# A state-space scan with a running attention behind it: attention in two halves, VectorE's side work between product and scan, decays six states ahead

## The chip, the cores and the metric

One core of one Trainium2 chip runs the whole program in one launch. The metric is the device time of an execution in microseconds. The core has five engines that run side by side and meet through semaphores: TensorE (PE in the profile, matmuls; PEld is its weight load), VectorE (DVE), ScalarE (ACT), GpSimd (POOL) and SyncE (SP), which here issues all transfers. All of them take their instructions in the order of the program.

## What is computed

The input x is 16 images of 128 channels by 64 x 64 positions. Layer 0 adds a selective state-space block (Mamba) to it, layer 1 an attention over prefixes, and after it a layer of experts. Cut to what matters here:

```python
u = group_norm(x) as tokens                      # 16 x 4096 x 128
xs, z = split(u @ W_in)
xc = silu(causal_conv(xs))                       # 256 channels, 4 taps
dt, Bm, Cm = split(xc @ W_xproj)                 # 8, 16 and 16 columns
delta = softplus(dt @ W_dt + b_dt)
A = -exp(A_log)                                  # 256 x 16
# over the 4096 tokens, for each channel d and each of 16 states n:
#   h[n] = exp(delta * A[n]) * h[n] + delta * xc * Bm[n]
#   y    = sum over n of h[n] * Cm[n]
x = x + ((y + xc * D) * silu(z)) @ W_out         # with rows and columns of the image swapped
t = x as tokens
k, v = silu(layer_norm(t) @ W_kv.T)              # 8 heads of 128
s = q . k                                        # one score per head and token
m = running max of s;  e = exp(s - m)
t = t + mean over heads of cumsum(e * v) / cumsum(e)
t = t + expert layer (top 8 tokens per expert)
```

## The kernel before

Each image has 4096 tokens; the kernel takes them in blocks of L = 512, 8 blocks to an image, 128 blocks in all. One step k of the main loop (line 600) works on four blocks at once: it scans block k (`cur`), finishes block k-1 (`prev`: gate, output projection, residual), prepares block k+1 (`nxt`: convolution, x projection, delta), and runs the attention of block m = k - 9 (`LAG`, line 566), whose image is then complete. `mp_` is the attention block of the step before, `mn` that of the next. So the first nine steps have no attention, and after step 127 some ten steps have attention alone.

A step has 16 slots n, one for each state. In a slot, `scan` (line 343) makes on DVE the product `bx` of delta times x (`du`) with row B of state n, in PSUM, and then two linear scans of 512 tokens (two halves of the channels) into `h`; POOL multiplies h with row C of the state into the tile of the decay (`da`); two slots later PE turns this tile by an identity and sums it in PSUM (`add_y`, line 364). The rows B and C come from memory, repeated over the partitions, by a transfer `load_bc` four states ahead (line 332, four buffers). `decay` (line 337) makes exp(delta * A[n]) on ACT, up to `LEAD` = 5 states ahead, in eight buffers. `keep_state` (line 358) copies the last token's state on ACT; h has two buffers.

Everything else of a step is spread over the slots by `slot(n)` (lines 611 to 703), an order written by hand: the wrappers `PE`, `DVE`, `ACT`, `POOL` (class `InOrder`, line 23) keep each engine's instructions in the order in which the code calls them. Transfers go through `nc.sync` and are placed by the framework's scheduler. In a slot the order is: scan, load_bc, the state copy of the slot before, `slot(n)`, `add_y(n-2)`, decays, loads.

The attention of a block: `ln_center`, `ln_scale`, `ln_apply` normalise; `key` makes one head's keys; `score` the scores in the one bank of pool `acc`; `score_max` the running max and four copies of rows into `lh`; `score_exp` e; `score_sum` the running sum and e turned into `e1`; `score_log` the logarithm of the sum and eight copies of rows into `rh`; `value` half the heads' values for one chunk of 128 tokens; `weights` (line 511) forms from lh and rh, by a matmul of 5 rows and an Exp on ACT, the 128 x 128 weights of a chunk for all heads; `attend` multiplies them with the values into `o` (pool `acc` again) and sums the chunk for `carry`; `attend_before` adds what comes from earlier chunks; `finish` adds the result to the image and stores it. PSUM has three banks for short results (pool `ps`), one for scores and o, two for y and two for bx.

In the slots before: keys 0 to 2, score_max 3, score_exp 4, score_sum 5, score_log 6, values 7 to 9, ln_center 10, weights of chunks 0 to 3 in slots 11 to 14 and attend of chunks 0 to 2 in 12 to 14, attend of chunk 3 and finish in slots 0 and 1 of the next step. `gate` is in slot 3, `residual` in 5, `delta_x` (du of the next block) in slot 15 behind the scan, `gn_stats` in 12, and `gn_end`, a short chain through DVE, PE and ACT, in slot 14 of one step in eight.

Of the kernel before, what the change touches and what calls it, by code (L numbers as in the profile page):

```python
# [39 lines left out]
def conv_attn_hybrid(ctx: ExitStack, tc: tile.TileContext, x, w_in, conv_w, conv_b, w_xproj, w_dt, b_dt,  # L40
# [72 lines left out]
    with ExitStack() as st:  # L113
# [94 lines left out]
        dap = st.enter_context(tc.tile_pool(name="dap", bufs=8))  # L208
# [133 lines left out]

        def scan(k, n):
# [5 lines left out]
            bt, da = w.pop(("bc", n)), w["da", n]  # L349
            bx = bps.tile([P, NH2, L], F32, tag="bx", name="bx")  # L350
            DVE.tensor_tensor(bx, w["du"], bc(bt[:, 0:1, :], [P, NH2, L]), ALU.mult)
# [55 lines left out]

        def residual(k):

            w = blocks.pop(k)  # L410
            J = L // HH
            xv = res[w["b"]].rearrange("p (i j) -> p j i", j=WW)[:, w["i"] * J : (w["i"] + 1) * J, :]
            DVE.tensor_tensor(xv, xv, w["o"].rearrange("p (j i) -> p j i", j=J), ALU.add)
# [6 lines left out]
        def ln_center(m):  # L420
            b, i, xs = where(m)
            s = att[m] = dict(cen=bank("cen_ps"))
            PE.matmul(s["cen"], cmat, xs, start=True, stop=True)
            s["sq"] = short("sq")
            ACT.activation(s["sq"], s["cen"], AF.Square)
# [9 lines left out]
        def ln_apply(m):  # L435
            s = att[m]
            s["xn"] = a1.tile([P, L], F32, tag="xn", name="xn", bufs=2)
# [18 lines left out]
        def score_max(m):  # L456
# [10 lines left out]

            for u in range(2):
# [9 lines left out]
        def score_sum(m):  # L478
# [4 lines left out]
            DVE.tensor_copy(gn[b]["den"], s["mx"][:, L - 1 : L])  # L483
            et = bank("et_ps")
# [38 lines left out]
        def attend(m, c):  # L523
# [3 lines left out]
            if c == 0:  # L527
                s["o"] = acc.tile([P, L], F32, tag="acc", name="ao_ps")
            cols, v, wm = bass.ts(c, P), s.pop(("v", c)), s.pop(("wm", c))
            for h in range(HD):  # L530
                g, j = divmod(h, 4)

                PE.matmul(s["o"][:, cols], v[:, h, :], wm[:, j // 2, j % 2, g, :], start=(c == 0 and h == 0),
# [16 lines left out]
        def attend_before(m, c):  # L550
            s = att[m]
            if m % NBLK or c:
                PE.matmul(s["o"][:, bass.ts(c, P)], carry[:, (c - 1) % 4, :], s["e"][:, bass.ts(c, P)], start=False,
                          stop=True, skip_group_check=True)

        def finish(m):
            b, i, xs = where(m)
            s = att.pop(m)
            DVE.scalar_tensor_tensor(xs, s["o"], 1.0 / HD, xs, ALU.mult, ALU.add)
            nc.sync.dma_start(t2_d[b, :, bass.ts(i, L)], xs)  # L560
# [6 lines left out]
        LEAD = 5  # L567
# [30 lines left out]
        decays(0, 0, 5)  # L598

        for k in range(NK + LAG + 1):  # L600
# [10 lines left out]
            def slot(n):  # L611

                if n == 0:
                    if mp_ is not None:
                        attend(mp_, 3)
                        attend_before(mp_, 2)
# [4 lines left out]
                    if mp_ is not None:  # L621
                        carry_on(mp_, 2)
                if n == 1:
                    if mp_ is not None:
                        attend_before(mp_, 3)
# [4 lines left out]
                    if mp_ is not None:  # L630
                        carry_on(mp_, 3)
                        finish(mp_)
                    if m is not None:
# [14 lines left out]
                if n == 3:  # L648
# [4 lines left out]
                    if prev is not None:  # L653
                        gate(prev)
                if n == 4:
                    if prev is not None:
                        out_proj(prev)
                    if m is not None:
                        score_exp(m)
                    if nxt is not None:  # L660
                        conv(nxt, 0)
                if n == 5:
                    if prev is not None:
                        residual(prev)
                    if m is not None:
                        score_sum(m)
                    if nxt is not None:
                        conv(nxt, 1)
                if n == 6 and m is not None:
                    score_log(m)  # L670
                if n == 7:
                    if nxt is not None:
                        conv_silu(nxt)
                    if cur is not None:
                        gate_silu(cur)
                    if nxt is not None:
                        xproj(nxt)
                if 7 <= n <= 9 and m is not None:
                    for x in ((0, 1), (2, 3, 4), (5, 6, 7))[n - 7]:
                        value(m, x // 2, x % 2)  # L680
                if n == 9 and nxt is not None:
                    delta(nxt)
                if n == 10:
                    load_exp()
                    if mn is not None:
                        ln_center(mn)
                if n == 11 and mn is not None:
                    ln_scale(mn)
                if m is not None:
                    if 11 <= n <= 14:  # L690
                        weights(m, n - 11)
                    if n >= 12:
                        c = n - 12
                        if c < 3:
                            attend(m, c)
                        if c == 1:
                            attend_before(m, 0)
                            carry_on(m, 0)
                        if c == 3:
                            attend_before(m, 1)  # L700
                            carry_on(m, 1)
                if n == 13 and mn is not None:
                    ln_apply(mn)

            for n in range(N):
                if cur is not None:
# [6 lines left out]
                    if n == N - 1 and nxt is not None:  # L713
                        delta_x(nxt)
                if prev is not None and n == 0:
                    keep_state(prev, N - 1)
                slot(n)
                if cur is not None and n >= 2:
                    add_y(cur, n - 2)
                if 3 <= n <= 6 or n >= 10:  # L720
# [4 lines left out]
                if n == 0 and i == 1 and cur is not None:  # L725
# [166 lines left out]
```

## Time and profile before

| what | value |
|---|---|
| median of 3 runs | 13192.64 us (13183.42 to 13194.23) |
| the profiled execution | 13180.11 us, span 13178.4 us |
| PE busy | 11484.8 us (87%), mean granted clock 0.886 |
| DVE busy | 9947.5 us (75%) |
| ACT busy | 7080.3 us (54%) |
| POOL busy | 6336.2 us (48%) |
| first du of the loop, last du | 72.3 us, 11108.1 us |
| HBM | 105 GB/s over the span |

The main loop ends near 11,190 us, attention alone runs to about 11,690, and the expert layer takes the rest; the change touches only the main loop and the steps behind it. Line numbers are of little use in the profile: all in-order instructions are recorded in the helper's line 31, so groups are told apart by their tiles (`out<-in`). A few per cent of the records are missing. The costliest groups, each a line of the page's fifth part: the multiply with C on POOL (2048 of 2946 ns), the scans on DVE (4096 of about 1260 ns), the products bx on DVE (2048 of 1509 ns), the decays on ACT (4096 of 711 ns), and on PE the turns of y (16384 of 287 ns), the attention's products (8192 of 336 ns) and the weights (2048 of 728 ns).

### The profile page before, as it was taken

How to read it: one execution, taken by the hardware profiler on the slowest of the kernel's cores; microseconds unless marked ns; L12 is line 12 of the kernel's file. 1: busy time of each engine (PE TensorE's matmuls, PEld its weight loads, DVE VectorE, ACT ScalarE, POOL GpSimd, SP SyncE). 2: the span in 40 equal slices, each digit the busy share in tenths (PEclk: the TensorE clock that was granted, in tenths of full speed). 3: DMA queues.
4: the chain of work that ended last, by engine and by line, in shares of the span. 5: the costliest groups of instructions: out<-in, count | busy, mean ns of one | idle time of the engine just before them, and what ended most of it. 6: DMA issues, size and time to landing. Idle time of an engine off the chain costs nothing. (4 is left out here: it accounts for less than half of the span.)

```text
span 13178.4 us, 153074 instructions
## 1 busy us (share of the span) xinstructions
PE 11484.8 (87%) x55359; PEld 6609.2 (50%) x55359; DVE 9947.5 (75%) x8977; ACT 7080.3 (54%) x12594; POOL 6336.2 (48%) x2590
## 2 busy tenths in 40 slices
PE   5588989889888989898989889888988898988887
PEld 3344555555455545554555555545555555444464
DVE  7988888888888888888888888888888888124422
ACT  4456555656565655566555656565656565432210
POOL 5655555555555555555555555555555555012310
PEclk7689999999999999999989999999999999888975
DMA  4544444444444444444444444444444443011127
GB/s 129 125 112 106 111 106 114 109 107 109 110 108 111 107 106 113 106 113 106 112 103 113 109 109 107 112 109 107 110 105 113 102 112 96 7 48 45 52 81 290
DMA packets 693703, 1400.71 MB, mean 106 GB/s; under 512 B 51072, under 2 KB 89616, under 8 KB 684752
## 3 DMA queue, kind: packets, MB, share of 16 engines
q1 hardware_dynamic: 692944, 1390.92, 40.8%
q8 instruction: 436, 7.14, 0.2%
q14 instruction: 323, 2.65, 0.1%
HBM read 1294.25 MB, written 92.27 MB: 105 GB/s over the span
## 5 line engine op out<-in xcount | busy, mean ns | idle before, releaser
L31 POOL TENSOR_TENSOR da<-h,bct 128x1024 f32<-128x1024 f32 x2048 | 6034.0, 2946 | 5154.1 <-DVE h L31 1812.6
L31 DVE TENSOR_TENSOR_SCAN h<-da,state,bx 128x512 f32<-128x512 f32 x3584 | 4392.4, 1267 | 578.3 <-ACT state L31 389.5
L31 DVE TENSOR_TENSOR bx<-du,bct 128x1024 f32<-128x1024 f32 x2048 | 3090.6, 1509 | 43.8 <-DMA bct<-bcs 2.9
L31 ACT ACTIVATE da<-delta,a_neg 128x512 f32<-128x512 f32 x4096 | 2639.6, 711 | 365.2 <-PE y_ps L31 359.1
L31 PE MATMUL y_ps<-ident,da 128*128 128x128 f32 x16384 | 2280.9, 287 | 154.5 <-POOL da L31 153.5
L31 PEld LDWEIGHTS y_ps<-ident,da 128*128 128x128 f32 x16384 | 1957.4, 148 | 900.4 <-issue 635.3
L31 ACT ACTIVATE wm<-w_ps 128x512 f32<-128x512 f32 x1024 | 608.7, 594 | 1561.7 <-PE w_ps L31 1559.1
L31 PEld LDWEIGHTS ao_ps<-wm,v 128*128 128x128 f32 x8192 | 1268.4, 244 | 346.5 <-issue 346.5
L31 PE MATMUL ao_ps<-wm,v 128*128 128x128 f32 x8192 | 1369.3, 336 | 0.0
L31 PE MATMUL w_ps<-rh,lh 5*128 5x512 f32 x2048 | 1320.7, 728 | 0.0
L31 PE MATMUL xs_ps<-xb,wc 128*128 128x512 f32 x2048 | 987.5, 627 | 304.1 <-DVE xt L31 302.3
L31 PE MATMUL k_ps<-xn,wk 128*128 128x512 f32 x2048 | 988.4, 615 | 55.2 <-DVE carry L31 55.2
L31 ACT ACTIVATE kt<-k_ps 128x512 f32<-128x512 f32 x1024 | 586.9, 602 | 755.3 <-PE k_ps L31 755.3
L31 PE MATMUL v_ps<-wv,xn 128*128 128x512 f32 x2048 | 964.9, 605 | 6.6 <-ACT z L31 3.3
L31 ACT ACTIVATE v<-v_ps 128x512 f32<-128x512 f32 x1024 | 610.4, 598 | 477.1 <-PE v_ps L31 477.1
L107 POOL TENSOR_SCALAR diag<-ident,rstd 128x128 f32<-128x128 f32 x512 | 299.1, 602 | 1164.5 <-DVE rstd L96 1100.1
L31 PEld LDWEIGHTS xs_ps<-xb,wc 128*128 128x128 f32 x2048 | 402.0, 202 | 797.6 <-issue 438.8
L31 DVE TENSOR_TENSOR_SCAN h<-da,bx 128x512 f32<-128x512 f32 x512 | 597.0, 1208 | 88.4 <-ACT state L31 60.1
L31 DVE TENSOR_TENSOR carry<-carry,carry_ps 128x128 f32<-128x128 f32 x496 | 135.9, 274 | 693.0 <-PE carry_ps L31 693.0
L31 PEld LDWEIGHTS k_ps<-xn,wk 128*128 128x128 f32 x2048 | 367.8, 196 | 483.3 <-issue 451.5
L31 ACT COPY state<-h 128x2 f32<-128x2 f32 x1792 | 334.2, 187 | 487.0 <-DVE h L31 486.5
L31 PEld LDWEIGHTS v_ps<-wv,xn 128*128 128x128 f32 x2048 | 363.3, 192 | 453.2 <-issue 430.8
(163 smaller groups left out, 11528.7 us busy)
## 6 DMA issues: line engine op xcount, KB each, us to landing
bct<-bcs SPq DMA_DIRECT2D x2048, 512.0 KB
xs<-in_x_dram SPq DMA_DIRECT2D x128, 256.0 KB
xt<-in_x_dram SPq DMA_DIRECT2D x16, 2048.0 KB
t_d<-xt SPq DMA_DIRECT2D x128, 256.0 KB
t<-t_d SPq DMA_DIRECT2D x64, 512.0 KB
tc<-t_d SPq DMA_DIRECT2D x16, 2048.0 KB
out_dram<-tc SPq DMA_DIRECT2D x16, 2048.0 KB
xb<-in_x_dram SPq DMA_DIRECT2D x112, 257.5 KB
```

Of the source, the lines that this page charges most:

```text
L31: return lambda *args, **kw: self.tc.keep_in_program_order(f(*args, **kw))
L107: nc.gpsimd.tensor_scalar(diag[:, c, :], ident, rstd[:, k : k + 1], None, ALU.mult)
```

## The change

- The product of slot n is taken out of `scan` into `product`. A slot now runs: `before(n)` (only score_sum in slot 7), in slot 0 `delta_x`, the product, in slot 12 `gn_stats`, then `beside(n)` (the former `slot`), then the scans, load_bc and the state copy of the slot before. So the state copy of slot n-1 now follows ACT's work of slot n.
- Attention in two halves: chunks 0 and 1 keep slots 12 to 15 of their step; weights and attend of chunks 2 and 3 go to slots 3 to 5 of the next step. `o` holds two chunks at a time, `finish` runs twice (slots 0 and 7 of the next step), with two stores of 256 columns. The four copies into lh move to slot 5 (`spread_weights`), score_exp to 6, score_sum to 7, the turning of e to 8 (`turn_weights`), score_log with its eight copies to 11, values to slots 8 to 10.
- Convolutions go to slots 6 and 7, conv_silu to 7, gate_silu and xproj to 8, delta and ln_center to 11, the square to 12, ln_apply to 14, out_proj to 5, residual to 6. In the second block of an image the projected output is set aside by an ACT copy and added in slot 11, and the load of the image's residual starts in slot 7.
- Decays run up to six states ahead in nine buffers, in slots 3 to 7 and 12 to 15; xn has one buffer in place of two.

```diff
+        def product(k, n):
+            w = blocks[k]
+            bx = w["bx"] = bps.tile([P, NH2, L], F32, tag="bx", name="bx")
+            DVE.tensor_tensor(bx, w["du"], bc(w["bc", n][:, 0:1, :], [P, NH2, L]), ALU.mult)
...
-            bt, da = w.pop(("bc", n)), w["da", n]
-            bx = bps.tile([P, NH2, L], F32, tag="bx", name="bx")
-            DVE.tensor_tensor(bx, w["du"], bc(bt[:, 0:1, :], [P, NH2, L]), ALU.mult)
+            bt, da, bx = w.pop(("bc", n)), w["da", n], w.pop("bx")
...
+        def set_aside(k):
+            w = blocks[k]
+            o = short("o")
+            ACT.copy(o, w["o"])
+            w["o"] = o
...
-            if c == 0:
+            if c % 2 == 0:
                 s["o"] = acc.tile([P, L], F32, tag="acc", name="ao_ps")
-            cols, v, wm = bass.ts(c, P), s.pop(("v", c)), s.pop(("wm", c))
+            cols, v, wm = bass.ts(c % 2, P), s.pop(("v", c)), s.pop(("wm", c))
...
-        def finish(m):
+        def finish(m, half):
             b, i, xs = where(m)
-            s = att.pop(m)
-            DVE.scalar_tensor_tensor(xs, s["o"], 1.0 / HD, xs, ALU.mult, ALU.add)
-            nc.sync.dma_start(t2_d[b, :, bass.ts(i, L)], xs)
+            s = att[m] if half == 0 else att.pop(m)
+            xs = xs[:, bass.ts(half, L // 2)]
+            DVE.scalar_tensor_tensor(xs, s["o"][:, : L // 2], 1.0 / HD, xs, ALU.mult, ALU.add)
+            nc.sync.dma_start(t2_d[b, :, i * L + half * (L // 2) : i * L + (half + 1) * (L // 2)], xs)
...
-        LEAD = 5
+        LEAD = 6
...
+            def before(n):
+                if n == 7 and m is not None:
+                    score_sum(m)
+            def beside(n):
                 if n == 0:
...
                     if m is not None:
                         key(m, 0), key(m, 1), key(m, 2)
                     if mp_ is not None:
-                        carry_on(mp_, 2)
+                        finish(mp_, 0)
...
+                    if mp_ is not None:
+                        weights(mp_, 2)
                 if n == 4:
+                    if mp_ is not None:
+                        weights(mp_, 3)
+                        attend(mp_, 2)
+                if n == 5:
+                    if m is not None:
+                        spread_weights(m)
                     if prev is not None:
                         out_proj(prev)
+                    if mp_ is not None:
+                        attend(mp_, 3)
+                        attend_before(mp_, 2)
+                        carry_on(mp_, 2)
+                if n == 6:
                     if nxt is not None:
                         conv(nxt, 0)
+                    if mp_ is not None:
+                        attend_before(mp_, 3)
                     if prev is not None:
+                        set_aside(prev) if i == 1 else residual(prev)
+                    if mp_ is not None:
+                        carry_on(mp_, 3)
+                    if m is not None:
+                        score_exp(m)
+                if n == 7:
+                    if mp_ is not None:
+                        finish(mp_, 1)
                     if nxt is not None:
                         conv(nxt, 1)
                         conv_silu(nxt)
+                if n == 8:
                     if cur is not None:
                         gate_silu(cur)
+                    if m is not None:
+                        turn_weights(m)
                     if nxt is not None:
                         xproj(nxt)
...
+                if n == 11:
+                    if nxt is not None:
+                        delta(nxt)
                     if mn is not None:
                         ln_center(mn)
+                    load_exp()
+                    if m is not None:
+                        score_log(m)
+                if n == 12:
+                    if mn is not None:
+                        ln_square(mn)
+                        ln_scale(mn)
+                    if m is not None:
+                        weights(m, 0)
+                if n == 13:
+                    if m is not None:
+                        weights(m, 1)
+                        attend(m, 0)
+                        attend_before(m, 0)
+                if n == 14:
+                    if mn is not None:
+                        ln_apply(mn)
+                    if m is not None:
+                        attend(m, 1)
+                        carry_on(m, 0)
+                if n == 15 and m is not None:
+                    attend_before(m, 1)
+                    carry_on(m, 1)
...
             for n in range(N):
+                before(n)
+                if cur is not None:
+                    if n == 0 and k:
+                        delta_x(k)
+                    product(cur, n)
+                if n == 12 and stat is not None:
+                    gn_stats(*stat)
+                beside(n)
                 if cur is not None:
                     scan(cur, n)
...
                     if n:
                         keep_state(cur, n - 1)
-                    if n == N - 1 and nxt is not None:
-                        delta_x(nxt)
...
-                slot(n)
...
-                if 3 <= n <= 6 or n >= 10:
+                if 3 <= n <= 7 or n >= 12:
                     decays(k, n, 2)
```

## The prediction, made before the changed kernel was run

> **What bounds the kernel now.** First the page's busy shares by slice: VectorE (DVE) 8 tenths and TensorE (PE) 8 to 9 through the loop, so neither is full, and PE's granted clock hangs between 0.8 and 0.9. A mean over such a loop says little, so the second view is a table of windows: one step of the first batch, where attention does not run yet, and one full step (from one BATCH_NORM_STATS2 to the next).
>
> ```profile
> DVE  7988888888888888888888888888888888124422
> PEclk7689999999999999999989999999999999888975
> ...
> 5013.00:5098.00 85.00, 76.55 (x389) 43.66 (x389) 74.00 (x65) 52.54 (x96) 47.09 (x16) 0.93 0.51 110
> 211.00:284.00 73.00, 43.91 (x176) 27.65 (x176) 70.42 (x55) 35.01 (x64) 49.62 (x17) 0.71 0.50 125
> ```
>
> The columns are PE, PE weight load, DVE, ACT, POOL busy, then the clock. Without attention DVE is the bound (70.4 of 73). With it DVE works 74.0 of 85, PE 76.6.
>
> Third, DVE's timeline in an attention-free step, beside POOL's there:
>
> ```profile
> 212.49 1.20 DVE L31 TENSOR_TENSOR du<-delta,xc 128x1024 f32<-128x1024 f32 x1
> 213.72 3.25 DVE L31 TENSOR_TENSOR bx<-du,bct 128x1024 f32<-128x1024 f32 x1
> 217.11 2.45 DVE L31 TENSOR_TENSOR_SCAN h<-da,state,bx 128x512 f32<-128x512 f32 x2
> 219.59 1.23 DVE L31 TENSOR_TENSOR bx<-du,bct 128x1024 f32<-128x1024 f32 x1
> ...
> 231.03 1.26 DVE L31 TENSOR_TENSOR z<-yb_ps,z 128x512 f32<-128x512 f32 x2
> 232.21 2.61 DVE L31 TENSOR_TENSOR bx<-du,bct 128x1024 f32<-128x1024 f32 x1
> ```
>
> The product bx takes 1.23 us directly behind a scan, and 2.6 to 3.25 when other DVE work stands between. POOL's multiply (2.35 us alone, 3.22 when a product got in first) then starts ahead of the product and the product sits it out. That is the cost which the reordering attacks.
>
> Fourth, what PE waited for in the full step, and SyncE's queue there:
>
> ```profile
> PE xs_ps L31 <- DVE xt L31: 2.6, 1, 2.6
> PE z_ps L31 <- ACT xc L31: 2.4, 1, 2.4
> PE o_ps L31 <- DVE z L31: 1.8, 1, 1.8
> PE w_ps L31 <- ACT rstd L31: 0.7, 1, 0.7
> PE var_ps L31 <- ACT sq L31: 0.6, 1, 0.6
> PE yb_ps L31 <- ACT kt L31: 0.4, 1, 0.4
> ```
>
> ```profile
> 5069.43 1.28 SPq L497 DMA_DIRECT2D rh<-mx  x2
> 5075.95 0.36 SPq L335 DMA_DIRECT2D bct<-bcs  x1
> 5076.38 3.66 SPq L497 DMA_DIRECT2D rh<-mx  x6
> ```
>
> The PE waits sum to 8.5 us. The queue shows that eight rh copies cost about 5 us of issue, and that a bct load, which waits for POOL to free its buffer, holds up those behind it (5.2 us here, harmless, as the weights follow 14 us later).
>
> **PE's account of a step, before.** From starts to next starts in PE's timeline at full clock: 17 turns y of 0.87 = 14.8; 4 weight pairs (w) of 2.74 = 11.0; 4 attends with their carry sums, 1.88 + 0.58 = 9.8; keys 6.9, values 6.9, convolution 6.9; scores 2.0, out projection 1.8, yb 1.0, z 1.7, dbl 1.7, dt 1.9, cen 0.9, var 1.0, et 0.5, four carried products 0.9. Sum 69.6. With 8.5 of waits, 6.9 of the 85.0 are left for half clock: the granted 0.93 alone makes 85 x 0.07 = 6.0. So PE and its waits fill the step; DVE's 74 fit inside.
>
> **The change, part by part.**
>
> *Products first.* Without attention, z, the residual and bn_stats no longer stand ahead of a product: 1.38 + 1.38 + 1.98 = 4.7 us a step. du still does (now ahead of product 0), and the row above with du straight before a product is 3.25, so 2.0 stay. Nine steps (0 to 8) give -42. In full steps the saved lock time (bx rows of 3.20, 2.14, 3.19 in the step shown: 4.8, less the 2.0) is DVE's. DVE's own work falls to about 72 + 2, so it waits more for PE instead; I give it nothing.
>
> *Decays six ahead, nine buffers.* No DVE wait names a decay; "ACT state" is the tiny state copy, which frees an h buffer. Gain nothing. But the copy of state n-1 now stands behind ACT's whole work of slot n, where it stood ahead of it. Scan n+1 waits for it, and with that for PE.
>
> *Half of attention in the next step.* Removed at PE: the waits of xs (2.6), o (1.8) and rstd (0.7); the out projection now has weights and an attend ahead of it. Kept: the z wait moves to dbl. After the convolution ACT does Silu 0.7, state 0.2, table 1.28, decay 1.25, table 1.28, z 0.6, about 5.4, and PE holds 3.1 of work: 2.4 of wait. The two extra table loads are in this, by the row of 1.28 each.
>
> The Trainium skill's "ScalarE: Activation LUTs", section "What ACT_TABLE_LOAD costs", speaks against them: it counts about 2.66 us a switch, drain included. The trace puts the next activation 1.30 after the load's start; by the page this wait would be 5.2 instead of 2.4.
>
> *var.* PE's work between the first dt and var shrinks to dt, cen and two turns of 0.87. ACT needs, after the last value's Silu: table 1.28, two Softplus 1.3, table 1.28, Ln 0.63, Exp 0.63, state 0.2, square 0.6. Wait 2.6 (0.6 before).
>
> *rh, the main price.* score_log moves from slot 6 to 11, one slot ahead of the weights that read rh. In the built program SyncE's queue has a bct load (it waits for POOL's multiply of state 11), the xs load and the eight rh copies, in this order. Count from X, when ACT has copied state 7, which lies behind the Silus of the first two values and releases scan 9. DVE: scan 9 from X+0.3 to X+2.8, two more pairs of product and scan at 3.85 (their start-to-start in the rows) to X+10.5, product 12 to X+11.7. POOL 2.35: X+14.1. bct and xs 0.36 each: rh begins X+14.9. One copy each 0.61; the semaphore events of before put a landing 1.75 behind its issue; the fourth (upper half) lands X+18.5, the eighth X+21.0. PE from X: six values, three turns, dt, cen and var with its wait reach the first w at X+14.4. So PE waits 4.1, then 1.1 more for the second half: 5.2. Queued behind: turns y, both attends, and DVE's carry sum of chunk 0 in slot 14, which scan 14 now follows. Bounds: 0 (if SyncE were early, as now) and 9 (if all eight landed before the first w).
>
> *Around the step's edge.* Scan 15, du, product 0 with POOL in between: turns 14 and 15 wait 1.6; yb 1.1 (its bank hangs on a key's Silu, and ACT has the block's norm, skip and take_y between); the second w of slot 3 has one free bank, 0.85.
>
> Waits: 2.4 + 2.6 + 5.2 + 1.6 + 1.1 + 0.85 = 13.75 (8.5 before). Half clock: dbl 1.7 (its row is 3.39 at half clock), and around w, where PE idles 2.6 and 4.1 nearly in a row, some 3: 4.7. Step: 69.6 + 13.75 + 4.7 = 88.0.
>
> The skill's "TensorE: Matmul & The Clock Gate", Part 1, has the clock fall after an idle window of about 3.4 us. The trace halved it after a wait of 2.36 (dbl). By the page the dbl loss vanishes and the step is 86.3; the measurement decides.
>
> *Small ones.* A second finish: between the 128-column carry (0.27) and the 512-column one (0.69), 0.45 twice, +0.2 on DVE, hidden in its waits; exposed it costs 24 us in all. A second store, 0.36 to 0.57 on SyncE, idle there. set_aside, one ACT copy of 0.58 in eight steps, ahead of a wait of ACT. xn with one buffer: its readers end four slots earlier.
>
> **Sum.** Starts of du from step 16 on give, before: 87.1 mean in six steps of eight, 97.4 where gn_end comes (k mod 8 = 6), 84.1 in the next. After: 88.0; with gn_end PE is no longer behind, DVE's stall falls from about 10 to 4.2: 92.2; in k mod 8 = 7 the built queue has the rh copies behind POOL's multiply of state 13, two slots later, with scans that need no state copy: +4.8, so 92.8. Of steps 9 to 127: 89 x 0.9 = +80, 15 x -5.2 = -78, 15 x 8.7 = +130. With -42: +90. The nine or ten drain steps gain the overlap of two chunks and lose the exposed rh copies (about 6.7): 0, bounds -60 and +60. Span 13178.4 + 90 = 13268; the profiled run was 13180 and the median 13193, so 13285 in the measure of the runs.
>
> **Rivals.** *The rh copies arrive in time* (faster). For: with DVE free of the lock the scans may run early and POOL frees bct sooner. Against: scan 9 hangs on ACT. Then 5.2 and 3 of clock go, step 80 to 82; at 82: 89 x -5.1, 15 x -11, 15 x -2, -42: about 12,540. If half of it comes true, 12,900. Together 0.34. *PE falls to half clock over all of slots 12 to 14* (slower): four windows of 3.41, as around 5096 now, instead of two: +3.4 a step, x 119 = +400, 13,690; it decides once the two waits together pass about 5 us. Chance 0.14. *The order does not do what it says*: the products are still long, because DVE idles between scan and product; then the 42 are lost and DVE still fits inside PE's step: 13,330, chance 0.08, on my side.
>
> **Chances.** My case 0.44, with its own spread of 13,050 to 13,500 (PE's clock loss and the bound of 60 for the drain), of which 0.04 lie on the faster side and 0.07 near zero; the rivals 0.34, 0.14, 0.08. A change under 0.2% (26 us) is what a measurement of this kernel cannot tell from none. Faster 0.34 + 0.04 = 0.38, same 0.07, slower 0.33 + 0.14 + 0.08 = 0.55. Range 12,650 to 13,720: it takes in half of the first rival and the second.
>
> **What would show it.** Right: bx after z, the residual, bn_stats at 1.23, after du 3.2; PE's longest new wait in the loop at w_ps, named DMA rh (or what SyncE carried), 4 to 6 us a step; a carry wait of DVE in slot 14; steps near 88. Wrong: no such wait, PE busy over 80 of each step, and steps below 85.

## The result, and the profile after

| | before | after |
|---|---|---|
| median (runs beside each other) | 13188.03 us (13180.96 to 13194.23) | 14405.81 us (14377.62 to 14445.70) |
| ratio | | 1.0926, 95 % interval 1.0898 to 1.0954 |
| span of the profiled execution | 13178.4 us | 14444.0 us |
| mean granted clock of TensorE | 0.886 | 0.804 |
| mean step with attention (du to du, steps 17 to 126) | 88.07 us | 98.67 us |
| step without attention (steps 3 to 5) | 72.1 us | 67.0 us |
| last du; from there to the end | 11108.1; 2070 us | 12310.5; 2133 us |

The change made the kernel 9.3 % slower; the forecast was 0.7 % slower, with a range that ended 690 us below the measured time. The page of the changed kernel (part 1, two rows of part 2, two groups of part 5, whose columns are busy us and mean ns, then the idle time before them):

```profile
PE 12400.1 (86%) x55359; PEld 7007.4 (49%) x55359; DVE 9524.3 (66%) x9105; ACT 7447.5 (52%) x12865; POOL 6747.8 (47%) x2590
...
DVE  8977767777777767767667767767767767314432
...
PEclk6688888888888888888788888888888888778875
...
L31 DVE TENSOR_TENSOR bx<-du,bct 128x1024 f32<-128x1024 f32 x2048 | 2784.6, 1360 | 69.1 <-DMA bct<-bcs 3.2
...
L31 PE MATMUL w_ps<-rh,lh 5*128 5x512 f32 x2048 | 1880.3, 1014 | 737.7 <-DMA rh<-mx 630.4
```

DVE lost a tenth or more in most slices of the loop: it waits now. Its product bx got cheaper on average. PE's busy time grew by 915 us with the same matmuls, and the row PEclk says why: the clock is 0.8 where it was 0.9. The weight matmuls show both new prices, 1014 ns each (728 before) and 738 us of waiting (none before). The same row of the page before:

```profile
L31 PE MATMUL w_ps<-rh,lh 5*128 5x512 f32 x2048 | 1320.7, 728 | 0.0
```

DVE's timeline across the edge of two attention-free steps (start, duration, engine, line, operation) shows the part that worked as meant:

```profile
205.77 1.20 DVE L31 TENSOR_TENSOR du<-delta,xc 128x1024 f32<-128x1024 f32 x1
207.00 3.26 DVE L31 TENSOR_TENSOR bx<-du,bct 128x1024 f32<-128x1024 f32 x1
...
220.58 1.23 DVE L31 TENSOR_TENSOR bx<-du,bct 128x1024 f32<-128x1024 f32 x1
221.72 1.28 DVE L31 TENSOR_TENSOR z<-yb_ps,z 128x512 f32<-128x512 f32 x2
222.92 2.44 DVE L31 TENSOR_TENSOR_SCAN h<-da,state,bx 128x512 f32<-128x512 f32 x2
```

With z behind the product instead of ahead of it, bx takes 1.23 us; only the product behind du still takes 3.26.

What PE waited for (total us, times, longest):

```profile
PE w_ps L31 <- DMA rh<-mx: 630.4, 106, 10.1
PE dbl_ps L31 <- ACT z L31: 280.4, 118, 2.4
PE y_ps L31 <- POOL da L31: 274.9, 212, 4.9
PE var_ps L31 <- ACT sq L31: 261.6, 126, 2.9
...
PE w_ps L31 <- DMA xs<-in_x_dram: 91.1, 18, 5.6
```

Both rows of w_ps are one wait, for rh: where xs is named, the copies into rh stood behind that load in SyncE's queue, as its timeline in one step shows:

```profile
5377.50 4.09 SPq L335 DMA_DIRECT2D bct<-bcs  x2
5381.69 0.42 SPq L238 DMA_DIRECT2D xs<-in_x_dram  x1
5382.16 5.44 SPq L516 DMA_DIRECT2D rh<-mx  x8
```

So the waits came where the forecast put them. What it did not have is in PE's timeline of the same step, in slots 3 and 4, where PE does not wait for rh at all (idle time before a group in brackets):

```profile
5327.36 0.39 PE L31 MATMUL w_ps<-maskb,identb 128*128 128x512 bf16 x1
5327.68 1.12 PE L31 MATMUL w_ps<-rh,lh 5*128 5x512 f32 x2
5329.48 0.38 PE L31 MATMUL w_ps<-maskb,identb 128*128 128x512 bf16 x1 [0.69 <-ACT wm L31]
5329.79 1.12 PE L31 MATMUL w_ps<-rh,lh 5*128 5x512 f32 x2
5330.84 1.60 PE L31 MATMUL y_ps<-ident,da 128*128 128x128 f32 x8
5332.24 0.63 PE L31 MATMUL w_ps<-maskb,identb 128*128 128x512 bf16 x1
5332.80 2.07 PE L31 MATMUL w_ps<-rh,lh 5*128 5x512 f32 x2
```

In the middle of the turn of y, with no wait but 0.69 us two rows earlier, the clock halves: the next two weight matmuls take 2.07 us where those before it took 1.12. The records of the clock change only on a grid of 3.413 us (off it by at most 0.005 us in any of the traces). A table of windows on that grid (length, PE busy and its matmuls, PEld, DVE, ACT, POOL busy, PEclk, then DMA share and GB/s), the first four from slots 3 and 4, the others from slots 12 and 13:

```profile
5327.86:5331.27 3.41, 2.72 (x9) 0.93 (x9) 3.38 (x5) 0.92 (x2) 3.21 (x1) 1.00 0.52 138
5331.27:5334.68 3.41, 3.41 (x10) 1.41 (x7) 3.38 (x5) 2.81 (x6) 0.13 (x1) 0.50 0.44 132
5334.68:5338.10 3.42, 3.42 (x7) 1.35 (x7) 3.25 (x4) 1.24 (x4) 3.07 (x1) 0.50 0.11 43
5338.10:5341.51 3.41, 3.41 (x27) 3.15 (x29) 1.19 (x1) 3.41 (x8) 3.23 (x1) 0.50 0.60 126
5382.47:5385.88 3.41, 0.00 (x0) 0.00 (x0) 1.43 (x2) 0.80 (x2) 2.96 (x1) 0.50 0.79 198
5385.88:5389.30 3.42, 2.37 (x3) 0.60 (x3) 0.00 (x0) 0.29 (x1) 0.24 (x1) 0.50 0.17 63
5389.30:5392.71 3.41, 3.41 (x9) 1.77 (x9) 0.40 (x1) 1.47 (x4) 0.00 (x0) 0.50 0.62 123
5392.71:5396.12 3.41, 3.41 (x8) 1.03 (x6) 3.38 (x4) 2.22 (x5) 1.22 (x1) 0.50 0.00 0
5396.12:5399.54 3.42, 3.42 (x9) 1.73 (x8) 0.38 (x1) 1.48 (x4) 1.99 (x1) 0.50 0.06 17
5399.54:5402.95 3.41, 3.41 (x28) 2.85 (x27) 0.00 (x0) 3.41 (x8) 0.00 (x0) 0.50 0.67 137
```

Windows in which PE was busy to the last tenth (3.41 of 3.41) stay at half clock, one after the other, while they are full of weight matmuls; the window that holds attend (x27, x28) is the last at half. The rows `5*128` of the weight matmuls are the suspect: they use 5 rows of the array of 128.

**The account used below.** From PE's records and the clock's, each step with attention is split in three: time in which no matmul ran (waits), half of the matmul time that lay in windows at half clock (half clock), and the rest, the work at full clock. Before, this gives 71.7 + 9.0 + 7.3 = 88.1 us. After: 70.8 + 12.5 + 15.4 = 98.7. Of the 10.6 us that the step grew, 8.1 are half clock and 3.5 waits, while the work fell by 0.9.

### The profile page after: what moved, and what is told of

Read it like the earlier page. It is cut to its first block, busy times and chain, and to the rows that moved or that the text cites. A ratio compares the mean times of both kernels' runs of the same rounds, so it can differ in the third digit from the quotient of the medians.

```text
span 14444.0 us, 153723 instructions
## 1 busy us (share of the span) xinstructions
PE 12400.1 (86%) x55359; PEld 7007.4 (49%) x55359; DVE 9524.3 (66%) x9105; ACT 7447.5 (52%) x12865; POOL 6747.8 (47%) x2590
## 5 line engine op out<-in xcount | busy, mean ns | idle before, releaser
L31 POOL TENSOR_TENSOR da<-h,bct 128x1024 f32<-128x1024 f32 x2048 | 6445.5, 3147 | 5952.7 <-DVE h L31 3057.1
L31 DVE TENSOR_TENSOR bx<-du,bct 128x1024 f32<-128x1024 f32 x2048 | 2784.6, 1360 | 69.1 <-DMA bct<-bcs 3.2
L31 PE MATMUL y_ps<-ident,da 128*128 128x128 f32 x16384 | 2470.6, 300 | 279.0 <-POOL da L31 274.9
L31 PEld LDWEIGHTS y_ps<-ident,da 128*128 128x128 f32 x16384 | 2088.3, 155 | 1157.6 <-issue 677.5
L31 PE MATMUL w_ps<-rh,lh 5*128 5x512 f32 x2048 | 1880.3, 1014 | 737.7 <-DMA rh<-mx 630.4
L31 PEld LDWEIGHTS ao_ps<-wm,v 128*128 128x128 f32 x8192 | 1371.2, 260 | 440.2 <-issue 440.2
L31 PE MATMUL ao_ps<-wm,v 128*128 128x128 f32 x8192 | 1456.1, 351 | 0.0
L31 PEld LDWEIGHTS w_ps<-rh,lh 5*128 5x128 f32 x2048 | 450.4, 272 | 1286.4 <-DMA rh<-mx 507.1
L31 PE MATMUL xs_ps<-xb,wc 128*128 128x512 f32 x2048 | 925.3, 594 | 1.8 <-issue 1.8
L31 PE MATMUL w_ps<-maskb,identb 128*128 128x512 bf16 x1024 | 534.7, 522 | 84.3 <-ACT wm L31 81.6
```

The costliest lines, as they stand in the source:

```text
L31: return lambda *args, **kw: self.tc.keep_in_program_order(f(*args, **kw))
```

## The experiments

Medians stand beside runs of the kernel before on the same chip; the right half is the account, mean us of a step with attention. In the names, rh_early means that the copies into rh come in slot 7, w32, w64 and w128 how many rows the weight matmuls take, lead5 decays five states ahead. The mended_ versions are after_rh_early_w64 with one more edit, rh_early_turns is after_rh_early with one, best_y is rh_early_w128_lead5 with one.

| kernel | median us | ratio to before (95 %) | step | work | waits | half clock |
|---|---|---|---|---|---|---|
| before | 13188 | 1 | 88.1 | 71.7 | 9.0 | 7.3 |
| after | 14406 | 1.0926 (1.0898 to 1.0954) | 98.7 | 70.8 | 12.5 | 15.4 |
| after_w64 | 13760 | 1.0430 (1.0413 to 1.0448) | 93.3 | 71.3 | 12.7 | 9.2 |
| after_rh_early | 13093 | 0.9933 (0.9908 to 0.9958) | 87.2 | 71.2 | 6.4 | 9.7 |
| after_rh_early_w64 | 12310 | 0.9335 (0.9321 to 0.9349) | 81.3 | 72.0 | 7.5 | 1.7 |
| before_w64 | 12711 | 0.9642 (0.9628 to 0.9656) | 84.4 | 72.3 | 9.9 | 2.2 |
| after_w128_lead5 | 12944 | 0.9818 (0.9803 to 0.9833) | 86.6 | 69.5 | 14.4 | 2.7 |
| rh_early_turns | 12671 | 0.9612 (0.9596 to 0.9628) | 83.9 | 71.6 | 8.3 | 4.0 |
| rh_early_w32 | 12643 | 0.9587 (0.9567 to 0.9607) | 83.7 | 71.6 | 7.0 | 5.1 |
| mended_scan_order | 12557 | 0.9520 (0.9505 to 0.9534) | 83.0 | 71.7 | 8.6 | 2.8 |
| mended_lead5 | 12294 | 0.9326 (0.9312 to 0.9340) | 81.1 | 72.0 | 7.6 | 1.5 |
| before_products | 13319 | 1.0092 (1.0071 to 1.0113) | 89.6 | 71.8 | 8.9 | 8.8 |
| before_products_w64 | 12494 | 0.9480 (0.9464 to 0.9495) | 82.8 | 72.3 | 9.6 | 0.9 |
| before_w128 | 12640 | 0.9589 (0.9575 to 0.9604) | 84.0 | 69.8 | 11.6 | 2.6 |
| rh_early_w128_lead5 | 11931 | 0.9044 (0.9029 to 0.9059) | 78.4 | 69.4 | 7.6 | 1.4 |
| best_y | 11763 | 0.8920 (0.8907 to 0.8934) | 77.1 | 69.4 | 6.8 | 0.9 |

### Rows of the weights, and the wait for rh

Two theories for the half clock: A, the 5-row matmuls; B, the waits. Four kernels make a square with the two edits below.

```diff
 # after_w64, before_w64, after_rh_early_w64 (rows 5 to 63 of rh are zero)
-                rows = slice(64 * u, 64 * u + 5)
+                rows = slice(64 * u, 64 * u + 64)
 # after_rh_early, after_rh_early_w64: Ln and the eight copies in slot 7
+        def score_ln(m):
+            s = att[m]
+            ACT.activation(s["mx"], s["mx"], AF.Ln)
...
                     if nxt is not None:
                         conv(nxt, 1)
+                    if m is not None:
+                        score_ln(m)
+                    if nxt is not None:
                         conv_silu(nxt)
```

> The changed kernel, with the second matmul of each pair of weight matmuls taking 64 rows of lh and rh where it took 5. The 59 added rows of rh hold zeros, so the sum, the number of matmuls and of output columns are the same; only more rows of the array are in use. Theory A (the half clock comes from the 5-row matmuls: a window of 3.4 us that they fill counts as idle however busy TensorE is): the share of time at half clock between 1000 and 11,000 us falls from 36.7 % to under 20 %, the mean full step from 98.6 us to 86 to 91, the time to 12,900 to 13,500 us. Theory B (the half clock comes from the time in which TensorE waits: for the copies into rh, for z and for var): those waits are as they were, so the share stays over 32 % and the time within 1.5 % of 14,406 us.

> The kernel before, with 64 rows in the second matmul of each weight pair where it took 5. Theory A: the share at half clock falls from 16.9 % to 8 to 13 %, since only part of it lies by the weights, where each pair stands between two attends; the time falls by 2 to 4 % to 12,650 to 12,950 us. Theory B: share and time as before, 13,188 us within 0.5 %.

> The changed kernel, with the logarithm of the sums and its eight copies into rh moved from slot 11 to slot 7, so that they land some 25 us before the first weight matmul; the second exponential stays in slot 11. The wait for rh (630 us in all, 5.2 a step) goes in both theories. Theory A: the windows that two pairs of 5-row matmuls fill stay at half clock: the share stays over 28 % and the time is 14,406 - 620 and a little, 13,550 to 13,900 us. Theory B: the windows at half clock behind that wait go with it (18 us of half clock in a step back to about 7): the share is under 22 % and the time 12,600 to 13,200 us.

> Both edits: logarithm and copies in slot 7, and 64 rows. Theory A: wait and half clock both go: share under 17 %, full step 80 to 85 us, time 12,200 to 12,800 us, faster than the kernel before. Theory B: as with the early copies alone, within 1 %.

The share of time at half clock, 36.7 % after and 16.9 % before, came to 26.4 % with 64 rows, 22.5 % with early copies and 5.7 % with both; on the kernel before 64 rows brought it to 5.7 % (A's time came true there, its 8 to 13 % was too high). So neither theory alone holds. The rows cost 6.2 us of half clock a step with the wait and 8.0 without it; the wait for rh costs 6.1 us itself (12.5 to 6.4) and 5.7 of half clock behind it, 7.5 where the weights have 64 rows. A's forecast for 64 rows alone (12,900 to 13,500 us) missed by 260 us, and with the early copies alone B's time came true (13,093 us; its share, under 22 %, just not), a gain about twice what A gave them. Both theories took the wait and the rows as rivals. They work in turn: the wait drops the clock, and the weights behind it hold it down. Both edits together undo the whole loss and beat the kernel before (ratio 0.9335), so the loss sat in these two; this version (after_rh_early_w64) is called the mended one below.

Windows of the version with 64 rows and the wait kept, from the end of the wait on; the last row is from slots 3 and 4 a step later:

```profile
5324.16:5327.57 3.41, 2.11 (x3) 0.60 (x3) 0.00 (x0) 0.03 (x1) 0.00 (x0) 0.50 0.13 46
5327.57:5330.98 3.41, 3.41 (x8) 1.51 (x8) 0.14 (x1) 1.47 (x4) 0.00 (x0) 0.50 0.42 130
5330.98:5334.40 3.42, 3.42 (x9) 1.29 (x7) 3.39 (x3) 2.23 (x4) 0.85 (x1) 0.50 0.00 0
5334.40:5337.81 3.41, 3.41 (x7) 1.47 (x8) 0.76 (x2) 1.46 (x4) 2.36 (x1) 0.50 0.01 1
...
5365.12:5368.53 3.41, 3.41 (x15) 1.41 (x13) 3.38 (x7) 2.69 (x6) 1.23 (x1) 1.00 0.65 148
```

The same 64-row weights that keep a full clock (last row, filled to 0.51 by them) do not bring one back (0.59 in each of the three before). This asks for one count with two thresholds.

### All rows, and rows between

```diff
 # after_w128_lead5, rh_early_w128_lead5, before_w128: lh once for each half, zeros in the other half's rows
-        lh = wp.tile([P, L], F32, name="lh")
+        lh = wp.tile([P, 2, L], F32, name="lh")
...
         nc.vector.memset(lh, -1.0)
+        nc.vector.memset(lh[64:, 0, :], 0.0)
+        nc.vector.memset(lh[:64, 1, :], 0.0)
...
-                rows = slice(64 * u, 64 * u + 5)
-                PE.matmul(rp, lh[rows, bass.ts(c, P)], rh[rows, c].rearrange("p x t -> p (x t)"),
+                PE.matmul(rp, lh[:, u, bass.ts(c, P)], rh[:, c].rearrange("p x t -> p (x t)"),
 # rh_early_w32
-                rows = slice(64 * u, 64 * u + 5)
+                rows = slice(64 * u, 64 * u + 32)
 # lead5
-        dap = st.enter_context(tc.tile_pool(name="dap", bufs=9))
+        dap = st.enter_context(tc.tile_pool(name="dap", bufs=8))
...
-        LEAD = 6
+        LEAD = 5
...
-        decays(0, 0, 6)
+        decays(0, 0, 5)
```

> The changed kernel with its wait for rh kept, and the second matmul of each weight pair over all 128 rows (lh kept once for each half with zeros in the other half's rows; decays five ahead with eight buffers, which frees the room). With 64 rows a window at half clock that they fill for 0.4 to 1.0 of its length stayed at half clock in 99 of 100 cases, at full clock it stayed full. Theory A (a window counts the rows in use times the time, and coming back to full clock takes a larger count than staying there): 128-row weights bring the clock back in the window after the wait, the half clock costs 3 to 5 us a step where 64 rows left 9.2, full step 87 to 89.5, time 13,050 to 13,400 us. Theory B (after a wait the clock stays at half for some windows whatever runs): 13,760 us within 0.7 %.

> The version with early copies, with 32 rows in the second matmul of each weight pair, between 5 (13,093 us) and 64 (12,310 us). A count of busy time x rows / 128 in each window of 3.41 us splits the windows of ten runs: at full clock the next is at half when the count is under 0.45, at half clock the next is full when it is 0.80 or more. Theory A (the count is proportional to the rows): a window filled to 0.6 by 32-row matmuls counts 0.55 and stays at full clock; the half clock costs 1.7 to 3 us a step, 12,310 to 12,500 us. Theory B (64 rows or a base at half of the array is what matters, 32 count as few): half clock as with 5 rows, 9 to 10 us a step, 13,000 to 13,150 us.

With 128 rows the wait for rh is still there and even longer (929 us in all against 630), yet the half clock falls to 2.7 us a step. The windows behind the wait:

```profile
5337.43:5340.84 3.41, 1.01 (x2) 0.53 (x3) 0.00 (x0) 0.00 (x0) 0.00 (x0) 0.50 0.18 59
5340.84:5344.26 3.42, 3.42 (x8) 1.49 (x7) 0.00 (x0) 0.81 (x2) 0.00 (x0) 0.50 0.38 97
5344.26:5347.67 3.41, 3.41 (x19) 2.30 (x18) 2.24 (x2) 3.41 (x8) 0.00 (x0) 1.00 0.02 5
```

One busy window, 0.74 of it 128-row weights, and the clock is back. Theory A holds for it; its time (12,944 us) came out below A's range by 106 us, for a reason that the last experiments show.

The rule that fits all of this: count for each window the busy time, with the second weight matmul's part weighed by its rows / 128. At full clock the next window is at half if the count is under 0.45; at half clock it is full from 0.80. Over the 46,880 windows between 1000 and 11,000 us of all sixteen kernels this names the next window right in 99.0 % (from full clock) and 98.4 % (from half clock). The thresholds come from the first ten kernels; on four measured later (rh_early_w32, before_products, rh_early_w128_lead5, best_y) they name 98.7 % and 96.4 %. Busy time alone, with its best thresholds, reaches 97.5 % and 65.0 % over all. The rule is a fit to this kernel's main loop: behind it, in the expert layer of best_y, nine windows in a row from 10,265 us on stayed at half clock though TensorE shows as busy throughout; among their matmuls are 64 with a single output column. And the other matmul over few rows, dt's (8 rows), fills at most 0.56 of a window at full clock and less than 0.2 of any at half clock, so that the runs don't show whether it counts by its rows too. Among windows with PE busy for 95 % and more:

| rows | weights' share of the window | at full clock: fell | at half clock: stayed |
|---|---|---|---|
| 5 | 0.2 to 0.4 | 0 of 839 | 392 of 392 |
| 5 | 0.4 to 0.6 | 67 of 342 | 539 of 539 |
| 5 | 0.6 to 0.8 | 235 of 235 | 252 of 252 |
| 64 | 0.4 to 0.6 | 0 of 1286 | 165 of 166 |
| 64 | 0.6 to 0.8 | 0 of 421 | 115 of 115 |
| 128 | 0.6 to 0.8 | 0 of 143 | 0 of 33 |
| none | 0 | 7 of 20784 | 30 of 2369 |

The 32-row kernel landed between its theories (12,643 us and 5.1 us of half clock a step; A had 1.7 to 3, B 9 to 10). The count holds for it (6 of 28 windows fell at a share of 0.6 to 0.8, both of two over 0.8), but A's estimate used only the threshold for falling; at half clock 110 of the 110 windows with a share over 0.4 stayed there.

### What stands beside the weights

```diff
 # rh_early_turns, slot 4 (slot 13 in the same way)
-                        weights(mp_, 3)
                         attend(mp_, 2)
+                        weights(mp_, 3)
```

> The version with early copies and 5 rows (13,093 us; half clock costs 9.7 us a step), with attend put ahead of the next weights in slots 4 and 13, so that 128-row matmuls stand between two weight pairs, as in the kernel before. Theory A (a window goes to half clock by how much of it 5-row matmuls fill): the half clock costs 5 to 7.5 us a step as before (7.3), attend waits up to 1 us a step for the weights' exponential: 12,700 to 13,000 us. Rival (which work stands beside the weights doesn't matter, only how many 5-row matmuls there are in a step): 13,093 us within 0.7 %, or more by the new wait.

With 5 rows and the early copies kept, only the order of attend and weights changed: the half clock fell from 9.7 to 4.0 us a step (A: 5 to 7.5), the waits rose by 1.9, the time fell to 12,671 us, a little below A's range. The neighbours of the weights matter, not their number alone. In the kernel before, the first two of a block's four weight pairs stand behind each other with only a turn of y between, and an attend stands ahead of the third and of the fourth. The change has such a double pair twice in a step, in slots 3 and 4 and in 12 and 13.

### The other parts of the change

```diff
 # mended_scan_order: early copies and 64 rows, the product back beside its scans
-                    product(cur, n)
                 if n == 12 and stat is not None:
                     gn_stats(*stat)
                 beside(n)
                 if cur is not None:
+                    product(cur, n)
                     scan(cur, n)
 # before_products: the kernel before, product first; before_products_w64: 64 rows as well
+                if cur is not None:
+                    product(cur, n)
+                slot(n)
                 if cur is not None:
                     scan(cur, n)
...
-                slot(n)
```

> The version with early copies and 64 rows (12,310 us, full step 81.3, step without attention 67.0), with one part of the change undone: each product with B stands again directly before its two scans, behind VectorE's other work of the slot. Theory A (TensorE's work, waits and half clock set the full step, so VectorE's order pays only in the steps without attention): these nine steps go from 67.0 back to about 72.1, the full steps move by less than 1 us: 12,340 to 12,460 us. Theory B (VectorE's chain of products and scans is close behind, and its 0.15 us for each of 16 products stands on the path of the full step too): full steps 83.5 to 85, 12,620 to 12,800 us.

> The version with early copies and 64 rows, with the decays five states ahead and eight buffers as before. Theory A (the sixth state of lead hides nothing that is late): 12,310 us within 0.5 %. Theory B (with five ahead the scans of slots 12 to 15 wait for decays behind the second exponential and the weights' exponentials on ScalarE): 1 to 3 us a step, 12,430 to 12,670 us.

> The kernel before with one part of the change alone: each product ahead of VectorE's other work of the slot, that work between the product and the two scans; attention, decays and copies stay. Theory A (the part is worth to the kernel before what it was worth to the version with early copies and 64 rows: 5.1 us in each of nine steps without attention and 1.8 us in a full step): 12,900 to 13,020 us. Theory B (in the kernel before only the steps without attention gain, since TensorE's work and half clock set its full steps): 13,110 to 13,170 us.

> The kernel before with the products moved and 64 rows in the weights. 64 rows alone took 12,711 us. Theory A (the products' place is a gain, 3 to 5 us in each of nine steps without attention and 1 to 2 us in a full step, and the half clock turned it into a loss): 12,420 to 12,600 us. Theory B (the order itself is bad for the kernel before, through the state copies and the carried sums that then stand between product and scan): 12,700 us or more.

Undoing the products' place cost the mended version 247 us (12,557 us, between the theories): 5.1 us in an attention-free step (67.0 to 72.1), as A had it, and 1.8 in a full step, between A (under 1) and B (2.2 to 3.7). So VectorE's order does reach the full step, through waits (+1.1) and half clock (+1.0). The sixth state of lead is worth nothing: 12,294 against 12,310 us.

The same part alone on the kernel before was a loss of 0.9 %, against both theories: attention-free steps fell to 69.2, but half clock rose from 7.3 to 8.8 us a step, work and waits within 0.1. With 64 rows the same part is a gain, 12,711 to 12,494 us, as A expected. What moved the windows so that more of them fell in the first case was not looked into.

### How far it goes

> Early copies, 128-row weights, decays five ahead. 64 rows and five ahead took 12,294 us with 1.5 us of half clock in a step, most of it in windows in which dbl waits. Theory A (the rest of the half clock is from waits, not from the weights): 12,294 us within 0.5 %. Theory B (64-row weights still keep some windows at half): 1 us a step less, 12,130 to 12,230 us.

> Early copies, 128-row weights, decays five ahead, and in slot 8 the turn of product 6 into y moved from the end of the slot ahead of dbl's matmul, which waits 3.5 us a step for ScalarE to empty z's bank. Theory A (the turn, some 2.4 us of TensorE, fills that wait and the window no longer falls to half clock): 2 to 4 us a step, 11,850 to 12,080 us. Theory B (GpSimd's product for state 6 isn't ready that early, so the wait changes its name): 12,294 us within 0.7 %.

> The kernel before with 128-row weights. 64 rows alone took 12,711 us; in the changed kernel's versions a pair of 128-row weights took 0.6 us less between its starts than one of 64 rows (2.15 against 2.74), four pairs a step. Theory A (the same here): 119 x 2.4 = 285 us less, 12,350 to 12,480 us, still over the 11,931 us of the changed order with early copies. Theory B (the gain needs the changed order, TensorE waits elsewhere here): over 12,600 us.

The 128-row version took 11,931 us, below both theories. The half clock is as with 64 rows (1.4 against 1.5 us a step); the work itself fell by 2.6 us. One weight pair's half in the version with 64 rows, then in the one with 128 (PE's timeline):

```profile
5301.38 0.38 PE L31 MATMUL w_ps<-maskb,identb 128*128 128x512 bf16 x1
5301.69 1.12 PE L31 MATMUL w_ps<-rh,lh 64*128 64x512 f32 x2
5302.74 0.39 PE L31 MATMUL w_ps<-maskb,identb 128*128 128x512 bf16 x1
```

```profile
5324.99 0.39 PE L31 MATMUL w_ps<-maskb,identb 128*128 128x512 bf16 x1 [0.49 <-DVE z L31]
5325.22 1.02 PE L31 MATMUL w_ps<-rh,lh 128*128 128x512 f32 x2
5326.08 0.38 PE L31 MATMUL w_ps<-maskb,identb 128*128 128x512 bf16 x1
```

From mask to mask it is 1.36 us with 64 rows and 1.09 with 128, both at full clock. The median over more than 450 pairs is 2.74 against 2.15 us for the pair, 0.1 us at each of its six matmuls; 5 and 32 rows take 2.73 as well. Four pairs a step make 2.4 of the 2.6 us.

The Trainium skill, "TensorEngine Tiling (Array Packing)", "Key Properties", says that a change of the tiling mode drains TensorE. For the 0.1 us between a mask, which takes all rows, and a weight matmul over part of them that would fit. But from the first weight matmul of a half to the second, both over the same rows, it is 0.1 us longer too (0.533 against 0.429), so a change of mode alone doesn't explain it; the cause stays open.

On the kernel before, 128 rows gave only 71 us over 64: the work fell by 2.6 us there too, and the waits rose by 1.7 (a new one, 222 us in all or 1.9 a step, at carry_ps for DVE's carried sum), as B expected. So the shorter work pays in full only in the changed order, which with early copies and 128 rows is 709 us faster than the old order with 128 rows.

Its last edit moves the turn of y ahead of dbl in slot 8:

```diff
 # best_y
                         turn_weights(m)
+                    if cur is not None:
+                        add_y(cur, 6)
                     if nxt is not None:
                         xproj(nxt)
```

Against 11,931 us it gained 167 and came out below A's range, which was counted from 12,294: waits down 0.8, half clock 0.5 a step. PE's waits in it:

```profile
PE y_ps L31 <- POOL da L31: 345.5, 239, 4.9
PE dbl_ps L31 <- ACT z L31: 273.2, 118, 2.8
```

The wait at dbl fell from 374 us in all to 273, or by 0.85 us a step; with the half clock that is less than the 2 to 4 us a step expected.

## Why the forecast missed

**Half clock, the step that failed.** The forecast had it fall, from 6.9 us in the step that it took apart to 4.7: 1.7 behind dbl and "around w, where PE idles 2.6 and 4.1 nearly in a row, some 3". Measured: 15.4 (7.3 before). In the step shown, dbl's is one window, 1.7 as forecast. Around w it is 8.0 (half of the 16.0 us of matmul time in the five windows from 5385.88 on) instead of 3, because the weights behind the wait cannot bring the clock back. In slots 3 and 4 it is 5.1 (three windows) instead of nothing: there two 5-row pairs drop the clock with hardly a wait. The difference of 10.7 us over 119 steps is 1273 us; the span missed by 14444 - 13268 = 1176, since the other terms missed by little and either way.

The sign of it could be seen in the trace of before, in slots 12 and 13 of a step (columns as above):

```profile
5014.13:5017.54 3.41, 3.41 (x14) 1.67 (x15) 3.28 (x2) 3.36 (x7) 1.84 (x1) 1.00 0.80 168
5017.54:5020.95 3.41, 3.41 (x28) 2.77 (x28) 2.66 (x4) 2.17 (x5) 1.04 (x1) 0.50 0.56 184
5020.95:5024.37 3.42, 3.42 (x14) 1.36 (x13) 3.29 (x3) 0.62 (x2) 1.30 (x1) 1.00 0.18 58
5024.37:5027.78 3.41, 3.41 (x16) 3.27 (x16) 3.24 (x4) 1.88 (x4) 1.60 (x1) 0.50 0.55 97
```

Twice a window with PE fully busy, filled to 0.59 and 0.62 by 5-row weights, is followed by one at half clock. The forecast took the 6.9 us of half clock as what was left over, without asking what made it, and for the changed kernel counted half clock only behind waits. The second rival ("over all of slots 12 to 14") named the place and its condition, waits of over 5 us in a row, and this came true (2.03 + 4.79); its price of 3.4 us more a step was too small, since it knew of no cause in slots 3 and 4, and its 13,690 us was still 5 % short.

The forecast weighed the Trainium skill's "TensorE: Matmul & The Clock Gate", Part 1, which has the clock fall after an idle window of some 3.4 us and return after a busy one. The windows of 3.41 us are in the trace; but busy windows fell, and 1413 busy windows with 5-row matmuls did not bring the clock back. By the page the loss would have been smaller still.

**Waits: right.** Forecast 13.75 us a step, measured 12.5. Singly: rh 5.2 forecast, 6.1 measured ((630.4 + 91.1) / 119); dbl 2.4 and 2.38; var 2.6 and 2.08; the second w of slot 3, 0.85 and 0.69 (81.6 / 119); turns of y 1.6 and 1.0 ((274.9 - 153.5) / 119); yb 1.1 and 0.37. The queue on SyncE was as foreseen: a load of bct, xs, eight copies. The rival of copies in time did not come: no run of the order as it stands had them early, and with the copies moved it was 9.1 % faster than the changed kernel. (That rival's price has a slip: its four terms as listed add up to -691 us, about 12,500 us and not 12,540.)

**Work: nearly.** 69.6 forecast, 70.8 measured. The step with gn_end was 3.4 us over the others (101.32 against 97.95; forecast 4.2), the one behind it 2.4 (forecast 4.8).

**Products first: right in free steps, too low in full ones.** 67.4 forecast, 67.0 measured; in a full step "I give it nothing" was 1.8 us in the mended version.

**Decays six ahead: right**, nothing. The state copy behind ScalarE's other work makes DVE wait 1464 us in all (450 before) without naming the time: the mended version, with the same order, waits 620 and is the faster one.

**Drain: just past its bound.** 0 with bounds of 60 either way; the stretch behind the last du grew by 63 us.

## What to carry to other kernels

Before a schedule is moved, look for matmuls over few rows and see which windows of the clock they fill: a stretch in which TensorE is busy but mostly with such matmuls can halve the clock as a wait does, and behind a wait they keep it there. Adding zero rows up to 64 cost nothing at full clock here (2.74 us a pair against 2.73) and bought 3.6 % on the old kernel alone. A part of a change should be judged with the clock's loss taken out, since that loss turned the sign of one part.

## What the runs showed of the hardware

- TensorE's clock took only the values 0.5 and 1.0, on a fixed grid of 3.413 us, and in the main loop the thresholds, fitted to its windows, differ by direction: about 0.45 of a window's busy time, with the weight matmuls weighed by their rows, to keep full clock, 0.80 to return to it. Rows that hold zeros count: the 59 added rows of rh were zero.
- In the weight pairs each of the six matmuls cost 0.1 us more when the weights took 5, 32 or 64 rows than when they took 128 (0.533 against 0.429 us from the first weight matmul of a half to the second, 0.31 against 0.216 from mask to weight). Why is not shown.
